# A decoder layer: who squares and sums the keys in its cross attention

## The chip, the core and the metric

The kernel runs on one core of a Trainium2 chip. A core has a matrix engine (TensorE, PE in the profile; PEld is its weight load), a vector engine (VectorE, DVE), an activation engine (ScalarE, ACT), a general engine (GpSimd, POOL) and a queue that issues transfers (SyncE, SP). They work side by side, each in the order of its own list of instructions, and wait for each other through semaphores. Operands lie in SBUF; matrix products land in PSUM, which is held here as eight banks of 128 partitions by 512 float32 numbers. The metric is the device time of one execution in microseconds (us), as the median over several runs.

## The reference

A decoder layer in float32 over 16 sequences of 100 tokens with 512 channels: causal self attention, cross attention over 361 context rows for each sequence, and a mixture of eight experts with two chosen for each token; each followed by a layer norm. The change lies in the cross attention:

```python
def _rmsnorm(x, w, eps=EPS):
    xf = x.astype(jnp.float32)
    var = jnp.mean(xf * xf, axis=-1, keepdims=True)
    return (xf * jax.lax.rsqrt(var + eps)).astype(x.dtype) * w
q = (hidden_states @ Wq + bq).reshape(b, s, NH, HD).transpose(0, 2, 1, 3)
k = (encoder_hidden_states @ Wk + bk).reshape(b, se, NKV, HD).transpose(0, 2, 1, 3)
v = (encoder_hidden_states @ Wv + bv).reshape(b, se, NKV, HD).transpose(0, 2, 1, 3)
...
q = _rmsnorm(q, qn_w)
k = _rmsnorm(k, kn_w)
scores = jnp.einsum('bhsd,bhed->bhse', q, k) * scale
...
out = jnp.einsum('bhse,bhed->bhsd', probs, v)
```

There are 16 query heads and 4 key and value heads (NKV) of 128 channels (HD2). Each key row is scaled, head by head, by the inverse root of the mean of its squares. So for each of the 361 context rows of each of 16 batches, four sums of 128 squares are wanted.

## The kernel before

**Stages.** The program runs self attention (to about 190 us), its output projection with the query projection of the cross attention (to about 395 us), the cross attention itself (to about 1030 us), and then its output projection, the router and the experts.

**Products.** To keep float32 accuracy, operands are split into a high and a low part (`split`: ACT writes the high part, L137; DVE or POOL writes the rest, L140), and each product is taken three times (`mm3`, L145 to L147: high by high, high by low, low by high).

**The cross attention.** The context of a batch has three chunks of rows (`CH`: 128, 128 and 105). `kv_project(b, i)` makes the keys and values of chunk `i` of batch `b`: twelve products into a PSUM tile `pk` (128x512, one bank), an add of the bias into the SBUF tile `ks` on DVE (L697), twelve products into a tile `pv`, the split of `pv` (ACT L137, DVE L140), and then the squares: DVE takes, for each of four heads, the products of 128 channels with themselves and their sum (L706; each shows as a custom DVE instruction and a short one that reads the accumulator). `rms_scale` makes the inverse root out of the sums: a scaling on DVE (L185, tile `v_k`), Ln and Exp on ACT (L157 `a_k`, L158 `y_k`), four small steps on DVE (L165 to L169), and POOL multiplies `ks` by it (L717). `kv_turn` (L727) transposes `ks` into the PSUM tile `ptk`, which is split into `kT_h` (ACT) and `kT_l` (DVE).

For each batch and key head, a unit `(b, g)`, `x_scores` takes four query heads: three products into a tile `s`, a pass on DVE that adds the mask and finds the minimum (L746), Exp on ACT (L757), the inverse of the sum on DVE (L758) and the scaling on POOL (L759). `x_turn` transposes the probabilities of a chunk into `ptp` (L767) and splits them into `pT_h` (ACT) and `pT_l` (DVE); `x_attend` multiplies them with the values into `av`, and ACT copies the finished unit to `o` (L787), which is stored and read again in the next stage. Queries are read back from memory into `qf` and split (`x_load`). Every third unit also loads and splits a row of the output weights (`f_wo`).

**What sets the order.** The loop over units (from L862) names the work of unit `(b, g)` beside the projection of chunk `g` of batch `b + 1` (for `g` of 0 to 2) and the transposes of the chunks made before. The final order on each engine is not that of the code: the tile framework runs a scheduler at build time (`schedule_with_timeline_sim=True`), which places each instruction by its own estimate of durations.

**Buffers.** PSUM comes from one pool (L557) with two buffers for each of four names: "mm" (`pk` and `pv` in turn), "s" (scores), "t" (`ptk` and `ptp`) and "av". A new tile of a name may be written when the last reader of the buffer it takes is done. `ks` has two buffers in SBUF (pool `c_0`, L676); `ksq`, to which DVE wrote the squares (they are not used again), has one.

Of the kernel before, what the change touches and what calls it, by code (L numbers as in the profile page):

```python
# [9 lines left out]
FP = mybir.dt.float32  # L10
FR = mybir.dt.float32r
AF = mybir.ActivationFunctionType
ALU = mybir.AluOpType
AX = mybir.AxisListType
# [10 lines left out]
NKV, HD2 = 4, 128  # L25
# [37 lines left out]
def tile_decoder_layer(  # L63
# [28 lines left out]
    nc = tc.nc  # L92
# [3 lines left out]
    def pool(stack, name, bufs=1, **k):  # L96
        return stack.enter_context(
            tc.tile_pool(name=name, bufs=bufs, reuse_waits="tile", **k)
        )
# [6 lines left out]
    def bank(tag, shape, name):  # L106
        return ps[-1].tile(shape, FP, name=name, tag=tag)
# [4 lines left out]
    def pair(p, shape, name, tag=None, bufs=None):  # L112
        k = {} if bufs is None else {"bufs": bufs}
        tag = tag or name
        return Pair(
            p.tile(shape, FR, name=f"{name}_h", tag=f"{tag}_h", **k),
            p.tile(shape, FR, name=f"{name}_l", tag=f"{tag}_l", **k),
        )
# [14 lines left out]
    def split(dst, src, high=None, low=None):  # L133

        high, low = high or nc.scalar, low or nc.vector
        if high is nc.scalar:
            ins = nc.scalar.copy(dst.h, src)  # L137
        else:
            ins = high.tensor_copy(dst.h, src)  # L139
        low.tensor_tensor(dst.l, src, dst.h.bitcast(FP), ALU.subtract)  # L140
        return ins
# [7 lines left out]
    def mmk(out, a, b, n=KC):  # L149
        for k in range(n):  # L150
            mm3(out, a(k), b(k), k == 0, k == n - 1)
# [31 lines left out]
    def rms_scale(ss, p, n, name, p_=None):  # L183
        v = (p_ or small).tile([128, n], FP, name=f"v_{name}", tag=f"rms_v{n}")
        nc.vector.tensor_scalar(v[:p], ss, 1.0 / HD2, EPS_RMS, ALU.mult, ALU.add)  # L185
        return rsqrt(v[:p], p, n, name, p_=p_)
# [85 lines left out]
    for k in range(KC):  # L272
# [8 lines left out]
        out=causal,  # L281
# [240 lines left out]
    for k in range(KC):  # L522
        i = 4 * NU - 8 + k
# [152 lines left out]
    w0 = pool(c_l, "c_0", 2, side="right")  # L676
# [9 lines left out]
    def kv_project(b, i):  # L686
        c0, n = CH[i]
        if i == 0:
            K[b] = pair(w2, [128, NKV, SP], f"kT_{b}", tag="kT")
            nc.gpsimd.memset(K[b].h[:, :, SE:].bitcast(FP), 0.0)  # L690
            nc.gpsimd.memset(K[b].l[:, :, SE:].bitcast(FP), 0.0)
        ct = CT.pop((b, i))
        m = b * len(CH) + i
        pk = bank("mm", [128, D], f"pk2_{b}_{i}")
        mmk(pk[:n], lambda k: ct[:, k, :n], lambda k: wk[:, k, :])
        ks = w0.tile([128, D], FP, name=f"ks_{b}_{i}", tag="ks")
        nc.vector.tensor_tensor(ks[:n], pk[:n], bk_bc[:n], ALU.add)  # L697
        pv = bank("mm", [128, D], f"pv2_{b}_{i}")
        mmk(pv[:n], lambda k: ct[:, k, :n], lambda k: wv[:, k, :])
        VS[b, i] = spare[m % 6]  # L700
        split(VS[b, i][:n], pv[:n])
        kr = ks[:n].rearrange("p (h d) -> p h d", d=HD2)
        ss = small.tile([128, NKV], FP, name=f"kss_{b}_{i}", tag="kss")
        sq = w0.tile([128, HD2], FP, name=f"ksq_{b}_{i}", tag="sq", bufs=1)
        for h in range(NKV):
            nc.vector.tensor_tensor_reduce(  # L706
                out=sq[:n],
                in0=kr[:, h, :],
                in1=kr[:, h, :],
                scale=1.0,  # L710
                scalar=0.0,
                op0=ALU.mult,
                op1=ALU.add,
                accum_out=ss[:n, h : h + 1],
            )
        rs = rms_scale(ss[:n], n, NKV, f"k_{b}_{i}")
        nc.gpsimd.tensor_tensor(  # L717
            kr, kr, rs[:n].unsqueeze(2).to_broadcast([n, NKV, HD2]), ALU.mult
        )
        KS[b, i] = kr  # L720
# [77 lines left out]
    for i in range(len(CH)):  # L798
        if i == 2:
            split_ctx(0, 2)  # L800
        kv_project(0, i)
        kv_turn(0, i)
# [59 lines left out]
    for i, (b, g) in enumerate(order):  # L862
# [9 lines left out]
        if b + 1 < B:  # L872
            if g == 0:
                fetch_ctx(b + 1)
                split_ctx(b + 1, 0)
            if g < len(CH):
                kv_project(b + 1, g)
            if g + 1 < len(CH):
                split_ctx(b + 1, g + 1)
# [91 lines left out]
    def iota(p, shape, pattern, base=0, mult=0, name=""):  # L971
# [17 lines left out]
        out=before,  # L989
# [11 lines left out]
        out=lower,  # L1001
# [18 lines left out]
        out=earlier,  # L1020
# [809 lines left out]
```

## Time and profile before

| | us |
|---|---|
| median of 6 runs | 1401.82 (1400.55 to 1405.13) |
| the profiled execution | 1399.77 |
| its span, from first to last instruction | 1398.0 |

The busy time of the engines by stretch of the span, in us:

| stretch | PE | DVE | ACT | POOL | granted clock |
|---|---|---|---|---|---|
| 0 to 190 | 181.1 | 122.8 | 114.8 | 138.2 | 1.00 |
| 190 to 395 | 202.2 | 135.8 | 90.6 | 85.2 | 0.99 |
| 395 to 430 | 34.1 | 22.3 | 13.6 | 14.1 | 1.00 |
| 430 to 600 | 166.9 | 125.4 | 110.8 | 93.1 | 1.00 |
| 600 to 800 | 195.2 | 145.7 | 130.0 | 109.6 | 1.00 |
| 800 to 1000 | 194.4 | 144.5 | 128.1 | 109.4 | 0.99 |
| 1000 to 1030 | 29.9 | 14.8 | 14.7 | 13.9 | 1.00 |
| 1030 to 1398 | 325.8 | 228.1 | 155.7 | 150.2 | 0.97 to 0.93 |

The granted clock is the share of full speed that the power control gave TensorE. How the lines of the profile read: a group has its source line, engine and operation, then the tile written and the tile read (buffer numbers left out, so `pk` stands for all key chunks), the shapes, the count, the busy time with the mean of one in ns, and the idle time of the engine just before it with what ended that. In a list of waits, the waiting engine, line and tile stand before the arrow and the releaser after it, then the total in us, how often, and the longest. A timeline has the start in us, the duration, the engine, the line and the tiles. A row by tile or line gives the shortest, median and longest duration in ns and the first and last start. A line can be that of a helper: L137 and L140 are all splits, L145 to L147 all products.

### The profile page before, as it was taken

The numbers are of one execution on the slowest core, as the hardware profiler recorded it, in microseconds if no ns is written. First come the engines' busy times: TensorE is split into PE (matmuls) and PEld (weight loads), VectorE is DVE, ScalarE is ACT, GpSimd is POOL, SyncE is SP. The second block draws the span as 40 slices with busy tenths as digits, with TensorE's granted clock in tenths as the row PEclk, the third lists the DMA queues.
The fourth block names the chain that finished last, engine by engine and source line by source line (L and its number), as shares of the span: only waits on it lengthen the run. The fifth ranks groups of instructions, "written<-read, shape, count | busy, mean of one in ns | idle before, by whom it ended". The sixth has DMA issues, their size and how long they took to land.

```text
span 1398.0 us, 25131 instructions
## 1 busy us (share of the span) xinstructions
PE 1329.5 (95%) x7952; PEld 1101.6 (79%) x7952; DVE 939.4 (67%) x2932; ACT 758.2 (54%) x1899; POOL 713.6 (51%) x839
## 2 busy tenths in 40 slices
PE   8999989999999999999999999999999898899995
PEld 6888868888878888888888888888887676577783
DVE  5766576766556777777777776777654557764586
ACT  4666653444445666666666666656654232333456
POOL 6877763344245455555555555554554445532630
PEclk9999999999999999999999999999999999989997
DMA  5231154645452123323333123222445544678873
GB/s 161 73 94 49 58 158 117 140 102 118 91 106 63 48 69 75 73 71 78 77 70 74 46 72 76 72 71 50 112 113 168 175 170 154 193 218 248 292 245 132
DMA packets 197872, 159.79 MB, mean 114 GB/s; under 512 B 133322, under 2 KB 152878, under 8 KB 197742
## 3 DMA queue, kind: packets, MB, share of 16 engines
q1 hardware_dynamic: 187904, 137.83, 35.9%
q0 software_dynamic: 4576, 14.95, 3.5%
q10 hardware_dynamic: 5262, 5.41, 1.3%
q8 instruction: 65, 1.06, 0.3%
q14 instruction: 65, 0.53, 0.1%
HBM read 107.16 MB, written 50.99 MB: 113 GB/s over the span
## 4 chain that ended last, share of the span: by engine, by line
PE 71%; DVE 14%; DMA 7%; ACT 4%; issue 3%; POOL 1%; SPq 1%; ACTq 0%; DVEq 0%; POOLq 0%
PE pq L145 4%; PE pq L147 4%; PE pq L146 4%; PE pv L145 4%; PE pv L146 4%; PE pv L147 3%; PE ptp L767 3%; PE pk L145 3%; PE pk L147 3%; PE pk L146 3%; PE s L145 3%; PE s L146 2%; PE s L147 2%; PE av L146 2%; DMA f_e<-in_expert_w 2%
## 5 line engine op out<-in xcount | busy, mean ns | idle before, releaser
L759 POOL TENSOR_SCALAR p<-p,sums 100x361 f32<-100x361 f32 x256 | 146.9, 579 | 99.7 <-DVE sums L758 88.8
L757 ACT ACTIVATE p<-p,nm 100x361 f32<-100x361 f32 x256 | 153.2, 601 | 40.2 <-DVE nm L746 36.9
L746 DVE CUSTOM_DVE_ANT_0 p<-s,nmask 100x361 f32<-100x361 f32 x256 | 132.9, 527 | 60.9 <-PE s L147 52.2
L140 DVE TENSOR_TENSOR pT_l<-ptp,pT_h 128x400 fp32r<-128x400 f32 (+1 forms) x192 | 107.5, 567 | 56.2 <-ACT pT_h L137 55.6
L145 PE MATMUL pq<-WH 128*128 128x512 f32 (+2 forms) x272 | 106.5, 392 | 5.3 <-DVE WH L139 5.3
L137 ACT CAST pT_h<-ptp 128x400 fp32r<-128x400 f32 (+1 forms) x192 | 91.4, 487 | 29.8 <-PE ptp L767 29.4
L767 PE MATMUL ptp<-ident,p 100*128 100x100 f32 (+1 forms) x768 | 107.1, 251 | 0.0
L140 POOL TENSOR_TENSOR cT_l<-cf,cT_h 128x512 fp32r<-128x512 f32 (+1 forms) x48 | 54.4, 1134 | 101.4 <-ACT cT_h L137 99.5
L767 PEld LDWEIGHTS ptp<-ident,p 100*128 100x128 f32 (+1 forms) x768 | 95.3, 151 | 13.3 <-POOL p L759 2.3
L146 PE MATMUL pq<-WL,WH 128*128 128x512 f32 (+2 forms) x272 | 104.0, 382 | 0.0
L147 PE MATMUL pq<-WH,WL 128*128 128x512 f32 (+2 forms) x272 | 103.7, 381 | 0.0
L147 PE MATMUL acc<-WH,ot_l 128*128 128x512 f32 (+1 forms) x208 | 86.2, 415 | 8.2 <-DVE ot_l L140 6.8
L145 PE MATMUL acc<-WH,ot_h 128*128 128x512 f32 (+1 forms) x208 | 85.8, 412 | 6.2 <-ACT ot_h L137 6.2
L145 PE MATMUL s<-kT_h,WH 128*100 128x362 f32 x256 | 87.7, 353 | 1.0 <-ACT kT_h L137 1.0
L145 PE MATMUL av<-pT_h,WH 128*128 128x400 f32 (+1 forms) x192 | 76.7, 399 | 8.3 <-ACT pT_h L137 8.0
L614 POOL TENSOR_TENSOR qs<-qs,r_q 128x512 f32<-128x512 f32 (+1 forms) x52 | 54.0, 1070 | 59.5 <-DVE r_q L169 49.1
L146 PE MATMUL acc<-WL,ot_h 128*128 128x512 f32 (+1 forms) x208 | 84.4, 406 | 0.0
L147 PE MATMUL s<-kT_h,WL 128*100 128x362 f32 x256 | 84.3, 329 | 0.0
L146 PE MATMUL s<-kT_l,WH 128*100 128x362 f32 x256 | 83.7, 327 | 0.0
L140 POOL TENSOR_TENSOR WL<-qf,WH 128x400 fp32r<-128x400 f32 x64 | 67.4, 1054 | 29.9 <-ACT WH L137 26.5
L145 PE MATMUL pv<-WH,cT_h 128*128 128x512 f32 (+1 forms) x192 | 78.7, 410 | 0.9 <-DVE WL L140 0.9
L145 PE MATMUL pk<-WH,cT_h 128*128 128x512 f32 (+1 forms) x192 | 77.3, 403 | 0.2
(337 smaller groups left out, 3995.2 us busy)
## 6 DMA issues: line engine op xcount, KB each, us to landing
qf<-qd SPq DMA_DIRECT2D x64, 200.0 KB, 2.8
of<-od SPq DMA_DIRECT2D x48, 256.0 KB, 3.6
cf<-in_ctxT SPq DMA_DIRECT2D x16, 722.0 KB, 4.3
eb<-in_expert_b SPq DMA_DIRECT2D x32, 256.0 KB, 4.1
ysd<-h SPq DMA_DIRECT2D x32, 256.0 KB, 4.2
f_e<-in_expert_w SPq DMA_DIRECT2D x30, 256.0 KB, 4.6
f_wq<-in_Wq SPq DMA_DIRECT2D x16, 256.0 KB, 3.3
f_wo<-in_Wo SPq DMA_DIRECT2D x16, 256.0 KB, 4.5
```

Source lines behind the costliest of these rows:

```text
L137: ins = nc.scalar.copy(dst.h, src)
L140: low.tensor_tensor(dst.l, src, dst.h.bitcast(FP), ALU.subtract)
L145: nc.tensor.matmul(out, a.h, b.h, start=start, stop=False)
L146: nc.tensor.matmul(out, a.h, b.l, start=False, stop=False)
L147: nc.tensor.matmul(out, a.l, b.h, start=False, stop=stop)
L614: nc.gpsimd.tensor_tensor(qr[:, hs, :], qr[:, hs, :], rs[:n, hs].unsqueeze(2).to_broadcast([n, GR, HD2]), ALU.mult,)
L746: nc.vector.tensor_tensor_reduce(out=p, in0=sc[:, :SE], in1=nmask, scale=1.0, scalar=BIG, op0=ALU.add, op1=ALU.min, accum_out=nm,)
L757: nc.scalar.activation(p, p, AF.Exp, bias=nm, scale=-1.0, accum_out=sh)
L759: nc.gpsimd.tensor_scalar(p, p, sh, 1.0, ALU.mult, ALU.mult)
L767: nc.tensor.transpose(pt[:n, h, :], probs[h][:, c0 : c0 + n], ident[:S, :S])
```

## The change

The bias add, the projections and everything behind the sums stay. The squares of all four heads are taken by ACT in one operation over 512 channels, from `ks` in SBUF into the tile `pk`, whose products the add has read by then; DVE then sums them head by head in one reduce from PSUM. The SBUF tile `ksq` goes.

```diff
         kr = ks[:n].rearrange("p (h d) -> p h d", d=HD2)
         ss = small.tile([128, NKV], FP, name=f"kss_{b}_{i}", tag="kss")
-        sq = w0.tile([128, HD2], FP, name=f"ksq_{b}_{i}", tag="sq", bufs=1)
-        for h in range(NKV):
-            nc.vector.tensor_tensor_reduce(
-                out=sq[:n],
-                in0=kr[:, h, :],
-                in1=kr[:, h, :],
-                scale=1.0,
-                scalar=0.0,
-                op0=ALU.mult,
-                op1=ALU.add,
-                accum_out=ss[:n, h : h + 1],
-            )
+        nc.scalar.activation(pk[:n], ks[:n], AF.Square)
+        nc.vector.tensor_reduce(
+            ss[:n], pk[:n].rearrange("p (h d) -> p h d", d=HD2), AX.X, ALU.add
+        )
         rs = rms_scale(ss[:n], n, NKV, f"k_{b}_{i}")
```

## The prediction

> **What bounds the kernel now.** I read the engine totals first, then the busy time of the stage that holds the change, then the waits of TensorE there, then timelines. The edit is in `kv_project`, whose DVE rows (L706) run from 398.7 to 993.7 us; so the stage is the cross attention, and I take 430 to 1000 us as its steady part.
>
> ```profile
> PE 1329.5 (95%) x7952; PEld 1101.6 (79%) x7952; DVE 939.4 (67%) x2932; ACT 758.2 (54%) x1899; POOL 713.6 (51%) x839
> 430.00:1000.00 570.00, 556.47 (x3151) 475.49 (x3150) 415.63 (x1579) 368.90 (x999) 312.03 (x427) 1.00 0.29 70
> PE av L145 <- ACT pT_h L137: 8.0, 11, 1.6
> PE av L146 <- DVE pT_l L140: 4.0, 19, 0.5
> PE s L145 <- ACT kT_h L137: 1.0, 2, 0.6
> ```
>
> The columns of the second line are PE, PEld, DVE, ACT and POOL. PE is busy 556.5 of 570 us at a granted clock of 1.00, DVE 73%, ACT 65%. PE sets the pace: its named waits sum to 13.0 us. A matmul that waits while the one before it drains shows only part of its wait, so I also took the step from each PE start to the next and compared it with the tenth-percentile step between the same two kinds of rows: the excesses over 0.12 us sum to 27.9 us. By the time since the last `ptk` transposes of 105 rows (the third key chunk; they return every 39 us, once per batch): 11.0 us at 36 to 40 us, just before they return; 7.0 at 8 to 10 us, behind casts of `f_wo`; 9.9 scattered. These 27.9 us are all that a lighter DVE can win in this stage.
>
> **The change part by part.** The rows of the removed and of the nearest added work:
>
> ```profile
> L706 DVE CUSTOM_DVE_ANT_0 ksq<-ks 128x128 f32<-128x128 f32 x112 | 44.1, 394 | 1.3
> L706 DVE CUSTOM_DVE_ANT_0 ksq<-ks 105x128 f32<-105x128 f32 x60 | 23.0, 384 | 0.5
> L603 ACT ACTIVATE qsq<-qs x52: 618/632/634, 213.7 to 395.3; 128x512 f32<-128x512 f32 x48, 64x512 f32<-64x512 f32 x4
> L604 DVE TENSOR_REDUCE qss<-qsq x52: 669/685/690, 214.4 to 396.0; 128x4 f32<-128x512 f32 x48, 64x4 f32<-64x512 f32 x4
> ```
>
> *Removed on DVE:* in the stage 67.1 us of products and, with 172 accumulator reads of some 80 ns, 13.8 us more: 80.9 us. *Added:* for each of 43 chunks one reduce of 128x512. The trace has none from PSUM; L604, from SBUF, takes 685 ns, and the add L697, of the same size from PSUM, also 683. I take 0.69: 29.6 us. DVE falls from 415.6 to 364 us, 64%. *Added on ACT:* one Square of 128x512; L603 (to SBUF) takes 632 ns, L1548 (a Square into PSUM, in the last stage) 602. I take 0.62: 26.7 us, so ACT rises to 69%. None of these busy times is a gain or loss in itself, since PE is the bound; they count where PE waits.
>
> The removed products have a median of 292 ns and a maximum of 1184. The Trainium skill, "SBUF — State Buffer", section "Who interferes with whom", says that a DVE instruction with two SBUF inputs can be shut out by a GpSimd instruction reading SBUF and that a reduce never is; the long rows agree. By that rule the reduce stays at the price above and the sum does not move.
>
> *The bank.* This is what the diff does not say. `pk` and `pv` share two PSUM banks (tag "mm"). Before, the bank of `pk` is free after the add L697; now the squares are written into it, and it is free only after the reduce. In the built order, three times per batch step a projection takes a bank that a `pk` held: `pv` of chunk 0 (its `pk` is chunk 2 of the batch before, far back), `pk` of chunk 1 (from chunk 0) and `pv` of chunk 1 (from its own `pk`). The second is tight already:
>
> ```profile
> 647.51 0.51 PE L767 MATMUL ptp<-ident,p 100*128 100x100 f32 x4
> 647.80 0.48 PE L145 MATMUL pk<-WH,cT_h 128*128 128x512 f32 x1
> 646.88 0.69 DVE L697 TENSOR_TENSOR ks<-pk,bk_bc 128x512 f32<-128x512 f32 x1
> 647.55 0.52 DVE L746 CUSTOM_DVE_ANT_0 p<-s,nmask 100x361 f32<-100x361 f32 x1
> 647.99 0.68 DVE L140 TENSOR_TENSOR kT_l<-ptk,kT_h 128x512 fp32r<-128x512 f32 x1
> 647.74 0.52 ACT L137 CAST WH<-qf 128x400 fp32r<-128x400 f32 x1
> 648.15 0.59 ACT L787 ACTIVATE o<-av,bvT 128x400 f32<-128x400 f32 x1
> ```
>
> The add ends at 647.57 and PE starts `pk` of chunk 1 at 647.80. The add cannot go earlier by much: there are two `ks` tiles, and it waits for the `ptk` transposes of the tile it reuses (started 646.02). In the new order ACT's Square stands behind the `qf` cast, so it starts at 648.15 and ends at 648.77; DVE does the score pass and `kT_l` first (next start 648.59), then the reduce from about 648.83 to 649.52; PE may start at about 649.6. PE's new order puts one group of four transposes (`ptp`, 0.29 us from start to start) ahead of `pk`, so PE arrives at 647.80 + 0.29 = 648.09. **Stall 1.5 us.** From below: add end 647.57 + 0.60 + 0.67 + three handovers of 0.05 = 649.0, a stall of 0.9; from above, one more operation of 0.6 in front: 2.1. I take 1.5, as the queues of the rows give it. Behind the stalled `pk`, PE's queue holds all attention work of the next units. On ACT, `o` and the next `pT_h` stand behind the Square; they are due only after `pk`'s twelve products (2.8 us), which cover them.
>
> *`pv` of chunk 1.* Before, it stands between the first score products (which need `kT_h`) and their second ones (which need `kT_l`) and covers `kT_l`. The new order puts the second ones first. With the rows of the same batch: the first ones start at 654.57 and issue until 654.96, `kT_l` runs 654.59 to 655.17, so PE waits 0.25 us (bounds 0 and 0.6). Then two pairs of score products (0.66) and a group of transposes (0.29) bring PE to 656.17; Square (654.72 to 655.34) and reduce (655.40 to 656.09) are just done: no stall.
>
> So each of 14 batch steps (key chunk 1 of batches 2 to 15) gets 1.5 + 0.25 = 1.75 us: **+24.5 us**.
>
> *What goes.* After `pk` of chunk 1, PE now waits here:
>
> ```profile
> 651.40 0.21 ACT L157 ACTIVATE a_k<-v_k 128x4 f32<-128x4 f32 x1 [1.68 <-DVE v_k L185]
> 651.58 0.53 PE L767 MATMUL ptp<-ident,p 100*105 100x100 f32 x4
> 652.27 0.45 PE L145 MATMUL av<-pT_h,WH 128*128 128x400 f32 x1 [0.16 <-ACT pT_h L137]
> 652.88 0.45 PE L146 MATMUL av<-pT_l,WH 128*128 128x400 f32 x1 [0.15 <-DVE pT_l L140]
> ```
>
> ACT sat 1.68 us on `v_k`, which came after the four products on DVE, and `pT_h` stood behind it. In the new order that `pT_h` stands before `a_k`, its transposes before `pk`, and DVE has one reduce instead of four products: the 11.0 us of this place go wholly. Of the other 16.9 I let half go, 8.4, since PE's own new stall gives every engine 1.5 us per batch to catch up, while the waits for `f_wo` are a DMA's. **-19.4 us** (bounds 11.0 and 27.9). Before 430 us the projections of two batches run nearly back to back (PE 34.1 of 35 us busy) and a reduce fits under the 2.8 us of the `pv` between two `pk`: 0, bounds -2 and +2 (DVE rows stretched to 1.07 and 0.88 us there).
>
> A rule speaks against the form: the Trainium skill, "ScalarE: Activation LUTs", section "Step-by-step: what each stage is for", calls PSUM the lower-latency destination for an activation, with the caveat that it is only useful if TensorE doesn't need most of PSUM. The two Square rows agree on the first half (602 against 632 ns); by it alone 48 chunks would save 1.4 us of ACT time, by the caveat the bank costs more than that.
>
> *Sum:* +24.5 - 19.4 = +5.1 us: span 1398.0 to 1403.1, the profiled run's 1399.77 to 1404.9. The median of the six runs shown lies 2.05 us above the profiled run, so I forecast a median of **1407 us** (+0.4%).
>
> **The rivals.** *Faster: the bank is back in time to matter little.* Place: the Square on ACT before `pk` of chunk 1. If the lighter DVE gives the add at once and ACT has the `qf` cast behind it, the stall is the lower bound, 0.9, and the score products wait for nothing: 12.6 - 19.4 = -6.8, **1395 us**. It decides from a stall below 1.2 us (0.25 + 1.2 times 14 is about the 19.4 that goes). For it: DVE sheds 51 us. Against: the add is tied to `ptk`, not to DVE's load, and the Square's place in ACT's queue is fixed.
>
> *No change:* the new stall only takes the place of the old ones, 14 times 1.4 against 19.4: **1402 us**. For it: PE is 98% busy before, and waits of slightly lagging engines merge into one.
>
> *Much slower:* the old waits stay, because ACT at 69% now also waits in order for the add, as it does for `v_k` today, and delays `pT_h`. Only 8 of 27.9 us go: 24.5 - 8 = +16.5, **1418 us**. For it: 8.0 of PE's 13.0 us of waits are for ACT already. Against: the Square stands where ACT has a `pk` of 2.8 us ahead.
>
> **How the numbers follow.** Forecast 0.45, faster 0.25, no change 0.15, much slower 0.15. Range: stalls of 0.9 and 0 give 1395, and 1394 with half of the bound before 430 us; of 2.1 and 0.25, 32.9 - 19.4 = +13.5, give 1415; beyond these I leave some 2 in 10. A difference of 0.2% (2.8 us) is about what this kernel's measurement can tell. Slower by more: 0.55 (the forecast's upper part and the last rival); within it 0.20; faster 0.25.
>
> **What would show it.** Right: PE idle before `pk` L145, released by DVE's reduce of `kss`, 14 times about 1.5 us, and `av` waits far below 12 us. Wrong: that wait under 1 us or absent; `av` waits as large as before; a reduce of more than 0.8 us; or a change outside 395 to 1000 us.

## The result, and the profile after

| | before | after |
|---|---|---|
| median, us | 1403.31 (46 runs) | 1413.62 (20 runs) |
| the profiled execution, us | 1399.77 | 1411.18 |
| its span, us | 1398.0 | 1409.0 |

The ratio is 1.0076, 95% interval 1.0062 to 1.0091: slower by 0.76%, or 10 us. That is about twice the forecast loss of 5.1 us; 1413.62 lies near the upper end of the range given, 1394 to 1415.

First the same two lines as before: the engine totals of the changed kernel's page, and its stage from 430 to 1000 us (PE, PEld, DVE, ACT, POOL, then the granted clock).

```profile
PE 1328.5 (94%) x7952; PEld 1105.2 (78%) x7952; DVE 916.4 (65%) x2596; ACT 780.5 (55%) x1947; POOL 711.0 (50%) x839
430.00:1000.00 570.00, 544.12 (x3096) 467.99 (x3094) 382.46 (x1254) 379.38 (x1017) 303.28 (x419) 1.00 0.28 67
```

PE does the same work in the whole program (1328.5 against 1329.5 us), but in the stage it idles 25.9 us of 570 instead of 13.5. DVE is lighter (382.5 against 415.6), ACT heavier (379.4 against 368.9).

Landmarks place the loss. The `ptk` transposes of the third key chunk return once per batch. From the second of them in the trace to the fifteenth, 13 batches, it takes 508.9 us before (460.53 to 969.45) and 517.9 after (460.57 to 978.43): 9.0 us. The next one, where the output stage begins to mix in, takes 1.6 us more, and what follows to the end 0.4. That is the 11.0 us of the span.

The waits of TensorE in the changed kernel from 395 to 1040 us (us in total, times, longest):

```profile
PE ptp L759 <- DVE kT_l L140: 11.3, 13, 0.9
PE av L145 <- ACT pT_h L137: 5.8, 4, 2.1
PE pk L145 <- DVE WL L140: 3.8, 4, 1.4
PE acc L145 <- ACT ot_h L137: 1.7, 1, 1.7
PE pk L145 <- DVE kss L705: 1.1, 4, 0.3
```

The first and the last line are missing from the list of before and belong to one place, the start of the projection of key chunk 1. The timeline of one batch there, in the changed kernel (rows of other work left out):

```profile
649.76 0.68 DVE L697 TENSOR_TENSOR ks<-pk,bk_bc 128x512 f32<-128x512 f32 x1
650.37 0.51 PE L759 MATMUL ptp<-ident,p 100*128 100x100 f32 x4
650.58 0.52 ACT L137 CAST WH<-qf 128x400 fp32r<-128x400 f32 x1
650.94 0.67 DVE L140 TENSOR_TENSOR kT_l<-ptk,kT_h 128x512 fp32r<-128x512 f32 x1
651.01 0.59 ACT L704 ACTIVATE pk<-ks 128x512 f32<-128x512 f32 x1
651.63 0.69 DVE L705 TENSOR_REDUCE kss<-pk 128x4 f32<-128x512 f32 x1
651.76 0.54 PE L759 MATMUL ptp<-ident,p 100*128 100x100 f32 x4 [0.88 <-DVE kT_l L140]
652.38 0.50 PE L145 MATMUL pk<-WH,cT_h 128*128 128x512 f32 x1
```

The add is done at 650.44, the Square stands behind the `qf` cast and ends at 651.60, the reduce ends at 652.32, and only then may PE write the bank: `pk` starts at 652.38. A group of four transposes takes 0.29 us from start to start, so without a wait `pk` would have started two groups after 650.37, at 650.95: the stall is 1.43 us. Over 14 batches it is 1.40 to 1.70, 20.9 us in all. Most of it is not shown at `pk`: the `ptp` group that was put ahead of it waits for its own bank first, while the Square and the reduce go on, so the list names `kT_l`. A reader who looked for `kss` alone would have found 1.1 us. The timeline also shows that the new order has a part of its own: behind `kT_l` this `ptp` group could not start before 651.76, whatever became of the bank, and `pk` not before 652.05. The bank is the later of the two; `sq_release` below shows it without that order.

### The profile page after: what moved, and what is told of

It is laid out like the page before. It is cut to its first block, busy times and chain, and to the rows that moved or that the text cites. A ratio compares the mean times of both kernels' runs of the same rounds, so it can differ in the third digit from the quotient of the medians.

```text
span 1409.0 us, 24865 instructions
## 1 busy us (share of the span) xinstructions
PE 1328.5 (94%) x7952; PEld 1105.2 (78%) x7952; DVE 916.4 (65%) x2596; ACT 780.5 (55%) x1947; POOL 711.0 (50%) x839
## 4 chain that ended last, share of the span: by engine, by line
PE 76%; DVE 10%; DMA 5%; ACT 4%; issue 3%; POOL 1%; SPq 1%; ACTq 0%; POOLq 0%; DVEq 0%
PE pq L145 4%; PE pq L147 4%; PE pk L145 4%; PE pq L146 4%; PE pv L145 4%; PE pv L147 4%; PE pv L146 4%; PE pk L147 4%; PE pk L146 4%; PE ptp L759 3%; DMA f_wo<-in_Wo 3%; PE s L146 3%; PE s L145 2%; PE s L147 2%; PE acc L145 2%
## 5 line engine op out<-in xcount | busy, mean ns | idle before, releaser
L137 ACT CAST pT_h<-ptp 128x400 fp32r<-128x400 f32 (+1 forms) x192 | 91.3, 486 | 54.6 <-PE ptp L759 53.4
L759 PE MATMUL ptp<-ident,p 100*128 100x100 f32 (+1 forms) x768 | 104.1, 252 | 12.4 <-DVE kT_l L140 11.3
L145 PE MATMUL av<-pT_h,WH 128*128 128x400 f32 (+1 forms) x192 | 72.9, 380 | 5.8 <-ACT pT_h L137 5.8
L147 PE MATMUL pv<-WH,cT_l 128*128 128x512 f32 (+1 forms) x192 | 76.0, 396 | 0.0
```

Source lines behind the costliest of these rows:

```text
L145: nc.tensor.matmul(out, a.h, b.h, start=start, stop=False)
L147: nc.tensor.matmul(out, a.l, b.h, start=False, stop=stop)
L759: nc.tensor.transpose(pt[:n, h, :], probs[h][:, c0 : c0 + n], ident[:S, :S])
```

## The experiments

Some chips of these runs needed 1416 to 1417 us for the kernel before, so results are ratios to it on the same chip, with their 95% interval. Beside them stand two numbers from each trace: the period of a quiet batch (one in which PE is not held up by a late row of `f_wo`), and the time of the same 13 batches. Both come from one execution per run, and that of before was on a chip where before needs 1403 us, so between chips the ratio is the safer number.

| run | quiet batch, us | 13 batches, us | ratio to before |
|---|---|---|---|
| before | 38.0 to 38.1 | 508.9 | 1 |
| after | 38.7 to 38.8 | 517.9 | 1.0076 (1.0062 to 1.0091) |
| sq_sbuf | 37.2 to 37.6 | 508.1 | 0.9948 (0.9930 to 0.9966) |
| sq_twice | 37.2 to 37.5 | 517.8 | 1.0003 (0.9981 to 1.0025) |
| mul_sbuf | 37.9 to 38.2 | 518.3 | 1.0035 (1.0013 to 1.0056) |
| mul_bank | 40.3 to 40.5 (its shortest) | 549.2 | 1.0233 (1.0210 to 1.0257) |
| hold | 38.8 to 38.9 | 529.7 | 1.0155 (1.0125 to 1.0185) |
| sq_release | 38.0 to 38.7 | 521.4 | 1.0053 (1.0028 to 1.0079) |
| before_early | 38.0 to 38.4 | 513.9 | 1.0009 (0.9991 to 1.0027) |
| after_early | 38.7 | 526.1 | 1.0069 (1.0046 to 1.0091) |
| sbuf_early | 37.2 to 37.6 | 513.6 | 0.9979 (0.9959 to 0.9999) |
| before_late | 38.0 to 38.2 | 498.7 | 0.9884 (0.9852 to 0.9916) |
| after_late | 38.7 | 506.8 | 0.9948 (0.9925 to 0.9970) |
| sbuf_late | 37.2 to 37.3 | 487.2 | 0.9793 (0.9765 to 0.9822) |

### The squares elsewhere

```diff
-        nc.scalar.activation(pk[:n], ks[:n], AF.Square)
+        sq = w0.tile([128, D], mybir.dt.bfloat16, name=f"ksq_{b}_{i}", tag="sq", bufs=1)
+        nc.scalar.activation(sq[:n], ks[:n], AF.Square)
         nc.vector.tensor_reduce(
-            ss[:n], pk[:n].rearrange("p (h d) -> p h d", d=HD2), AX.X, ALU.add
+            ss[:n], sq[:n].rearrange("p (h d) -> p h d", d=HD2), AX.X, ALU.add
         )
```

> The changed kernel, but ACT's Square writes a bf16 tile of 128x512 in SBUF (there is no room for an fp32 one) and DVE reduces from it; the order on PE is almost that of the kernel before. The bank theory (what costs is that pk's bank is held through Square and reduce, 14 times about 1.47 us): the waits of ptp and pk before chunk 1 (11.3 + 4.9 us) go, the 11.0 us that the lighter DVE freed stay freed, so the time is 1403.3 - 11 = 1392 us, ratio to before 0.992 (0.988 to 0.997). The ACT theory (what costs is the Square in ACT's queue and the chain add, Square, reduce across two engines): ACT has the same work as in the changed kernel, so 1409 us or more, ratio 1.004 or more. The order theory (what costs is the new order on PE as such): the order of before is back but nothing else is won, 1403, ratio 0.998 to 1.002.

The stage, PE's waits from 395 to 1060 us, and the same place of a batch in the timeline:

```profile
430.00:1000.00 570.00, 553.90 (x3153) 477.64 (x3153) 388.00 (x1276) 392.57 (x1043) 310.22 (x427) 0.99 0.30 70
```

```profile
PE s L145 <- ACT kT_h L137: 7.2, 4, 2.1
PE av L145 <- ACT pT_h L137: 7.1, 7, 2.0
```

```profile
651.05 0.51 PE L760 MATMUL ptp<-ident,p 100*128 100x100 f32 x4
651.34 0.48 PE L145 MATMUL pk<-WH,cT_h 128*128 128x512 f32 x1
```

ACT and DVE have the same operations as in the changed kernel (Square 630 ns, reduce 685 ns), yet `pk` starts 0.29 us after the transposes, no wait names `ptp` or `pk`, and the time falls below that of the kernel before. Square and reduce by themselves are not the cause of the loss, then, and the 0.998 to 1.002 of the order theory lie above the interval. What part of the changed kernel's loss came through its order stays open here, since the order went back together with the bank.

### A second Square

```diff
         nc.scalar.activation(sq[:n], ks[:n], AF.Square)
+        nc.scalar.activation(sq[:n], ks[:n], AF.Square)
```

> As the run with the squares in SBUF, but ACT takes the Square twice into the same tile: 43 more operations of about 0.62 us on ACT in the stage, and a chain from add to reduce that is 0.6 us longer. Bank theory: ACT (about 69% busy) takes them beside PE's work; at most 4 us above the run with one Square, ratio to before up to 0.996. ACT theory: each Square of a batch step costs what the change cost, about 11 us over 43 chunks, so at least 8 us above the run with one Square.

It is 0.55% above `sq_sbuf`, about 7.7 us: more than the bank theory gave (4), just less than the ACT theory asked (8); with these intervals the time alone excludes neither. The traces divide it: the quiet batches are the same (37.2 to 37.6 us), so the second Square costs nothing there. The 13 batches are 9.7 us longer, all of it in batches with a late `f_wo`, and some 8.5 us of that goes with the granted clock, which fell six times instead of twice (an estimated 11.9 us lost against 3.4; last section). The runs agree: their median granted clock is 0.973 against 0.9765, by estimate 5 us of the span. So no price of ACT's load is seen at the bank; whether it has one where it meets the wait for `f_wo`, or the clock fell by chance, these runs do not tell.

### The bank without ACT

> No Square on ACT: DVE squares the keys in one multiplication of 128x512 into a bf16 tile in SBUF and reduces from it (about 1.4 us of DVE per chunk against 1.9 before). Bank theory: like the kernel before or somewhat better, 1394 to 1403 us, ratio 0.993 to 1.000, the pre-ptk wait of pT_h partly there. ACT theory: faster than the run with ACT's Square in SBUF by the 26.7 us that ACT is spared, 1392 or less, while that run is at 1409 or more.

> No Square on ACT, but the bank held: DVE's one multiplication of 128x512 writes the squares into pk in PSUM and the reduce reads them there. Bank theory: the bank is back after add, multiplication and reduce with DVE's other work between, a stall of 1.5 to 2.2 us per batch as in the changed kernel or above it: 1410 to 1420 us, ratio 1.005 to 1.012. ACT theory: like the same products written to SBUF, 1403 us or less.

```diff
-        nc.scalar.activation(pk[:n], ks[:n], AF.Square)
+        nc.vector.tensor_tensor(pk[:n], ks[:n], ks[:n], ALU.mult)
```

This is `mul_bank`; `mul_sbuf` has `sq[:n]` in place of `pk[:n]`, as above. Neither has a Square on ACT, and they differ by 2.0% (28 us), as the bank theory said and the ACT theory did not; `mul_bank` is even above its range. Its named waits, from 395 to 1060 us, hardly show the bank:

```profile
PE av L145 <- ACT pT_h L137: 24.4, 23, 1.6
PE s L145 <- DVE nm L738: 11.1, 26, 1.6
```

Its built order has other work ahead of `pk`, and I read the waits of that work as the same late bank, paid for where the scheduler moved the hole; no run separates this. `mul_sbuf` missed its range (0.993 to 1.000): its quiet batches are those of the kernel before, with the same idle time of PE in the last 8 us before `ptk` of the third chunk, 0.35 us (before 0.33, `sq_sbuf` 0.17). Its loss of 0.35%, 5 us, lies in the batches with a row of `f_wo`; the median granted clock of its runs is 0.973 against 0.9775 for before on that chip, by estimate 6 us. One multiplication and one reduce on DVE do not help `pT_h` there; one Square on ACT and one reduce do.

### The bank alone

```diff
+        end = small.tile([128, 4], FP, name=f"kend_{b}_{i}", tag="kend")
+        in_turn(nc.vector.tensor_copy(end[:n], pk[:n, :4]), last)
```

Added to `sq_sbuf` behind its reduce (`last`); `in_turn` makes the scheduler keep one instruction behind another.

> The squares go to the bf16 tile in SBUF as in the run sq_sbuf, and one DVE copy of 128x4 that reads pk is put behind the reduce: all engines do the same work as in sq_sbuf but for some 0.06 us of DVE per chunk, and the bank is held as long as in the changed kernel. Bank theory: the gain of sq_sbuf turns into the loss of the changed kernel, quiet period 38.5 to 38.9 us instead of 37.2, ratio to before 1.004 to 1.012. ACT theory (Square in ACT's queue, handovers): as sq_sbuf, within 0.3% of its 0.995.

PE's waits in this run from 395 to 1060 us:

```profile
PE ptp L762 <- DVE kT_l L140: 11.4, 13, 0.9
PE av L145 <- ACT pT_h L137: 7.2, 5, 2.7
PE pk L145 <- DVE WL L140: 6.5, 4, 1.9
PE pk L145 <- DVE kend L710: 3.2, 13, 0.4
```

And the place in one batch (rows of other work left out):

```profile
662.55 0.69 DVE L706 TENSOR_REDUCE kss<-ksq 128x4 f32<-128x512 bf16 x1
663.15 0.15 DVE L710 COPY kend<-pk 128x4 f32<-128x4 f32 x1
663.36 0.50 PE L145 MATMUL pk<-WH,cT_h 128*128 128x512 f32 x1 [0.18 <-DVE kend L710]
```

Reading 4 of 512 columns of the bank late turns -0.5% into +1.6%. Taken as above, the stall before `pk` of chunk 1 is 1.44 to 1.80 us in each of 14 batches; in `sq_sbuf` it is 0 to 0.28. The copy takes 0.15 us, more than the 0.06 expected. The quiet period is 38.8 to 38.9 us, as expected, and `ptp` waits as in the changed kernel (11.4 us against 11.3, 13 times). The ratio lies above the range: the batches with a late `f_wo` are longer here (40 to 44 us, four falls of the clock), and the median granted clock of the runs is 0.9745 against 0.978 for before on that chip, by estimate 5 us. The order on PE also goes back to that of the changed kernel, with `ptp` ahead of `pk`: it follows from the late bank. This is the decisive run: the same Square and the same reduce, and the loss comes back with the bank.

### The bank for the Square only

```diff
-        nc.vector.tensor_reduce(
-            ss[:n], pk[:n].rearrange("p (h d) -> p h d", d=HD2), AX.X, ALU.add
-        )
+        nc.vector.tensor_reduce(ss[:n], kr, AX.X, ALU.max)
```

> The changed kernel, but DVE's reduce takes the maximum of ks in SBUF instead of the sum of the squares in pk, so the root mean square of the keys is left out; the Square is still written to pk and nobody reads it. So the bank is held by the Square only and comes back about 0.7 us earlier (a reduce of 0.69 us). Bank theory: 0.7 us less in each of 14 batches, 10 us below the changed kernel: ratio to before 1.000 (0.996 to 1.004), period of a batch without f_wo trouble 38.0 us instead of 38.7. ACT theory (Square in ACT's queue): as the changed kernel, 1.005 or more, period 38.5 or more.

Half a miss. By its time this run decides nothing: 1.0053 is what the ACT theory gave, and the interval overlaps that of the changed kernel. Of the quiet batches three are at 38.0 to 38.1 us and two at 38.7. The place itself tells more: two of PE's waits from 395 to 1060 us, and one batch (rows of other work left out).

```profile
PE ptp L757 <- DVE kT_l L140: 6.0, 7, 1.2
PE pk L145 <- ACT pk L704: 4.9, 6, 1.0
```

```profile
692.92 0.51 PE L757 MATMUL ptp<-ident,p 100*128 100x100 f32 x4
693.11 0.52 ACT L137 CAST WH<-qf 128x400 fp32r<-128x400 f32 x1
693.54 0.59 ACT L704 ACTIVATE pk<-ks 128x512 f32<-128x512 f32 x1
694.18 0.50 PE L145 MATMUL pk<-WH,cT_h 128*128 128x512 f32 x1 [0.75 <-ACT pk L704]
```

In seven of the 14 batches one group of `ptp` stands ahead of `pk`, as in the kernel before. The first of them has no stall; in the other six PE waits for the Square at `pk` itself, and the stall is 0.92 to 1.19 us, so the bank costs without the new order too. Over all 14 batches the stall is 13.9 us against 20.9 in the changed kernel. Leaving out the reduce gives back 0.5 us per batch, not 0.7: the Square behind the `qf` cast holds the bank for most of the time by itself. Of these 7 us the ratio shows 0.2%, 3 us, which the noise does not tell from nothing.

### The other wait: rows of f_wo

In the changed kernel 4 waits of `av` for `pT_h` and 4 of `pk` for `WL`, 9.6 us, stand behind ACT's cast of a row of `f_wo`. ACT's wait for that row's DMA, from 430 to 1000 us, before and after:

```profile
ACT WH L137 <- DMA f_wo<-in_Wo: 24.5, 16, 2.3
```

```profile
ACT WH L137 <- DMA f_wo<-in_Wo: 33.8, 16, 4.5
```

The first attempt issued the loads a unit earlier:

```diff
+        if i % 3 == 1 and 7 <= i < 7 + 3 * NKV * KC:
+            w, k = divmod((i - 7) // 3, KC)
+            fetch_row(f"wo_{w}", wo_slot[w], Wo4[w], k)
         if i % 3 == 2 and 8 <= i < 8 + 3 * NKV * KC:
             w, k = divmod((i - 8) // 3, KC)
-            load_row(f"wo_{w}", wo_slot[w], Wo4[w], k)
+            split_row(f"wo_{w}", k)
```

> The kernel before with the loads of wo's rows one unit earlier: the control for the two others. ACT's 24.5 us of waiting for f_wo's DMA go, batches with a row come from 39.0 to 40.6 us towards the quiet 38.0: ratio to before 0.993 (0.989 to 0.997).

> The changed kernel with the loads of wo's 16 rows issued one unit (about 10 us) earlier than their casts. In the trace of the changed kernel the batches with a late row of f_wo last about 1 to 3 us longer than the quiet ones, some 15 us in all. If the bank's stall and the wait for f_wo's DMA are two costs that add up: the quiet period stays at 38.7, the other batches come close to it, ratio to before 0.999 (0.994 to 1.003), and still 0.6 to 0.9% above the kernel before with the same early loads. If a stall of PE only gives other engines time that they need anyway (waits merge): the same as the kernel before with early loads, within 0.3%.

> Squares by ACT into the bf16 tile in SBUF, and the loads of wo's rows one unit earlier. Bank theory with the f_wo account: quiet period 37.2 us for all batches, without the 23 us by which the batches with a row of f_wo exceeded it: ratio to before 0.983 (0.978 to 0.989), about 1% below the kernel before with early loads. ACT theory: no better than the kernel before with early loads.

All three missed: nothing was won. ACT still waits for the DMA 16 times, 29.2 us in `before_early`: the scheduler, which decides the order, put the casts forward with the loads, and they start 4 to 5 us after them as before. So these runs do not tell whether the wait matters. The second attempt ties each cast behind the last `pT_h` of its unit:

```diff
-            split_row(f"wo_{w}", k)
+            in_turn(split_row(f"wo_{w}", k), PT[b, g, 2, 0])
```

> The kernel before, with the 16 loads of wo one unit earlier and each cast of f_wo tied behind the last pT_h cast of the unit, so that ACT no longer waits for the DMA (in before_early the scheduler had moved the casts forward together with the loads). The account by batches: quiet ones at 38.0 us with 0.3 us of PE idle, the others 1 to 2 us longer for ACT's wait. So all 13 batches come to 38.0 to 38.3: 509 to 494 to 498 us, ratio to before 0.991 (0.986 to 0.996). If ACT's wait for f_wo is not what lengthens those batches: 0.998 to 1.002.

> The changed kernel with the same late casts of f_wo. If the bank's stall and the wait for f_wo are separate costs that add up: all 13 batches at 38.7 to 39.1 us (a cast now stands ahead of a Square in one batch of three), ratio to before 0.998 (0.993 to 1.003), still 0.5 to 1.0% above before_late. If they merge: within 0.3% of before_late.

> Squares by ACT into the bf16 tile in SBUF, and the late casts of f_wo. Bank theory with the account by batches: 37.2 to 37.6 us for all batches, 13 of them 484 to 489 us instead of 509: ratio to before 0.983 (0.978 to 0.988). If neither the bank nor the wait for f_wo matters: 0.995 or more.

Now the casts start 11 to 17 us after their loads in `before_late`, ACT's wait for the row is gone in all three runs, and all three fell. The kernel before gains 1.2% by this alone. `after_late` is above `before_late` by 0.9948/0.9884 = 1.0065: the bank's loss stands beside the other and does not merge with it. And `sbuf_late` is 2.1% faster than the kernel before, 1385.66 us where that took 1415.59 on the same chip. Its stage and the only wait of PE that the list still names between 395 and 1060 us:

```profile
430.00:1000.00 570.00, 568.45 (x3269) 492.68 (x3268) 401.15 (x1310) 403.14 (x1067) 318.32 (x435) 1.00 0.32 74
```

```profile
PE pv L145 <- DVE WL L140: 1.4, 1, 1.4
```

PE is busy 568.5 of 570 us, and in the same window it ran 3269 rows against 3151 before.

## Why the prediction was right in sign and half in size

**What bounds the kernel: right.** With nearly all of PE's idle time in the stage gone, the time fell by 2.1% (`sbuf_late`). The idle time of a trace does not rank every run, though: `sq_sbuf` idles 16.1 us there and before 13.5, on different chips.

**The prices: right for each operation, wrong for the busy time.** The two rows of the changed kernel:

```profile
L705 DVE TENSOR_REDUCE kss<-pk x48: 677/691/694, 399.6 to 1004.0; 128x4 f32<-128x512 f32 x32, 105x4 f32<-105x512 f32 x16
L704 ACT ACTIVATE pk<-ks x48: 593/602/611, 398.9 to 1003.3; 128x512 f32<-128x512 f32 x32, 105x512 f32<-105x512 f32 x16
```

The prediction had 0.69 and 0.62 us, and no reduce was stretched. DVE fell by 33 us in the stage, not by the 51 that the sum of removed and added rows gives. Rows on DVE overlap, so their durations add up to more (507 us before) than the busy time (415.6): without the rows of L706 the rest of DVE is still busy for 362.2 us, so they held 53.4 us by themselves, not 80.9. It decided nothing, since DVE is not the bound.

**The bank: right.** Place, cause and size were as worked out: 1.49 us per batch against 1.5, 20.9 us against 21.0. The Square began behind the `qf` cast, the reduce behind the score pass and `kT_l`. Only the name in the list was wrong: `ptp` waits for `kT_l` and hides most of the wait for `kss`. The prediction's own sign, a wait before `pk` released by `kss` 14 times, did not come (4 times, 1.1 us in all), and by its letter that spoke against it; the timelines show the stall all the same. The second part of the term, 0.25 us per batch at the second score products, is about 1 us in all instead of 3.5. Together some 21.9 against 24.5.

**What goes: here it failed.** The forecast let 11.0 us just before `ptk` go "wholly" and, of the other 16.9 us, half: "since PE's own new stall gives every engine 1.5 us per batch to catch up". The loss in the stage, 10.6 us, leaves 21.9 - 10.6 = 11.3 us that went, not 19.4. The excess steps before `av`, taken as in the prediction, fell from some 22 to 12 us, and those just before `ptk` are gone. Of the other half nothing came. The batches show it: the quiet ones went from 38.0 to 38.7 us, and what the rest exceed them by is the same, 508.9 - 13 x 38.05 = 14.3 us before and 517.9 - 13 x 38.7 = 14.8 after. A stall of PE lets ACT catch up, but a cast that waits for a DMA is not made earlier by it; the prediction named that objection and then took half all the same. With the lower bound, 11.0, its own sum would have been +13.5 us and 1415. The prediction took the stalls 2.6 us too high and the gain 8.1 us too high. The two cancel in part: that its sum missed by some 5 us and not by 8 is luck.

**The rivals.** *Faster* needed a stall below 1.2 us; no batch had it. *No change* needed the stall to replace the old waits one for one; `before_late` and `after_late` show that they add. *Much slower* gave 1418, nearer to the 1413.6 measured than the forecast's 1407, and let 8 of the 27.9 us go where some 11 went. But it had them stay because of ACT's Square: the waits that stayed are those for `f_wo`, not the ones for `v_k`, and a second Square costs nothing in quiet batches.

## What to carry to other kernels

When an edit writes a scratch result into a PSUM tile that "is free anyway", price the time until its last reader is done against the next matmul that takes that bank: here the same edit with the scratch in SBUF was 0.5% faster than before, in the bank 0.8% slower. A stall is not always named after what holds it: work that was put into the hole shows its own, smaller wait. And let a wait go in a forecast only if its releaser comes earlier; one for a DMA does not, and needs its own cure.

## What was not expected of the hardware

Short pauses of PE can cost more than their length. The windows of `sbuf_early` around one wait (PE busy is the second number after the bounds, the granted clock the third from the end):

```profile
506.00:507.00 1.00, 0.66 (x4) 0.33 (x3) 0.00 (x0) 0.51 (x1) 0.59 (x1) 1.00 0.00 0
507.00:508.00 1.00, 0.00 (x0) 0.00 (x0) 0.16 (x1) 1.00 (x5) 0.81 (x1) 1.00 0.00 0
508.00:509.00 1.00, 0.71 (x2) 0.45 (x3) 0.89 (x2) 1.00 (x4) 1.00 (x2) 1.00 0.00 0
509.00:510.00 1.00, 1.00 (x7) 0.84 (x7) 1.00 (x4) 1.00 (x5) 0.01 (x1) 1.00 0.00 0
510.00:511.00 1.00, 1.00 (x4) 0.70 (x3) 1.00 (x5) 1.00 (x4) 0.96 (x1) 0.56 0.08 16
511.00:512.00 1.00, 1.00 (x4) 0.67 (x3) 0.91 (x5) 1.00 (x5) 0.69 (x3) 0.50 0.00 0
512.00:513.00 1.00, 1.00 (x4) 0.73 (x3) 0.16 (x1) 0.18 (x2) 1.00 (x2) 0.50 0.72 197
513.00:514.00 1.00, 1.00 (x4) 0.70 (x4) 0.00 (x0) 0.00 (x0) 0.61 (x2) 0.73 0.03 8
```

PE rests 1.47 us; about 2 us after it works again, the clock is halved for 3.4 us, although PE is busy: its `pk` products then start every 0.43 us instead of 0.24. By estimate, half of 3.4 us, that costs 1.7 us more. In the 14 traces there are 107 pauses over 0.9 us between 440 and 1000 us, and 35 such falls (three of them twice as long). Each fall begins during such a pause or at most 2.03 us after one; `before_late` and `sbuf_late` have no pause that long and no fall. Which of the pauses is punished looks like chance, and it makes part of the scatter between executions. The Trainium skill, "TensorE: Matmul & The Clock Gate", section "Why this matters for your kernels", asks for no idle gaps above about 3 us; here falls came with gaps of 0.94 to 2.74 us, about one gap in three, so for this kernel the measurement sets the stricter bound. Whether the clock looks at single pauses or at a share of busy time, these runs do not settle.
